# Logits turned one block later, and later loads spread over the run, in a float32 mixture-of-experts and mixing kernel on one core

## The chip, the cores and the metric

The kernel runs on one core of a Trainium2 chip. The metric is the device time of one execution in microseconds; less is better. Inputs and outputs are float32.

## The reference

x has 8 sequences of 512 tokens with 128 features. Three steps follow each other, each with a layer norm and a residual; the first and the third have the same weights.

```python
x = x + 0.5 * ffn(layernorm(x), centroids, expert_biases, Ws_up, Ws_down, W_up, W_down)
x = x + attn(layernorm(x), WB, WBf, w1, w2, b)
x = x + 0.5 * ffn(layernorm(x), ...)

def ffn(x, ...):                       # 64 experts, hidden width 64, 8 chosen
    shared = silu(x @ Ws_up) @ Ws_down
    aff = x @ centroids.T              # the logits
    idx = top_k(aff + expert_biases, 8)
    w = sigmoid(aff[idx]); w = w / (sum(w) + 1e-8)
    cw = zeros(T, E); cw[t, idx] += w  # weight of each expert for each token
    h = silu(einsum('td,edf->etf', x, W_up))
    y = einsum('etf,efd->etd', h, W_down)
    return shared + einsum('etd,te->td', y, cw)

def attn(u, WB, WBf, w1, w2, b):
    xf = u @ WB.T, but u itself at the first token
    xb = u @ WBf.T, but u itself at the last token
    gamma = sigmoid(xf @ w1.T + xb @ w2.T + b)
    return gamma * (xf + xb) + (1 - gamma) * u
```

## The kernel before

All experts are computed for all tokens. The work is a list of 16 items: layer 0 for sequences 0 to 7, then layer 1 (the mix of the reference's second step, and its third) for sequences 0 to 7. Each item has 32 pairs of experts, so there are 512 steps n, each called a block here, plus 25 in which only the down products are left. In a block the loop at L549 writes:

- the up product of pair n (`up`, L495): 128x128 weights of two experts with the 512 tokens, into one of four ph buffers in PSUM; ScalarE makes h of it by silu (L497). The products of blocks 5 and 7 go into the second PSUM pool, which y uses later (`SPARE`).
- a scaling (`scale`, L503) by VectorE of the h of 22, later 20, blocks ago with the cw of its two experts. cw comes from DRAM: for every group of four pairs two loads of 512 KB (L338), which repeat each expert's row over 64 partitions. Four groups have room (`CW_BUFS`); when a group's last pair is scaled, the load of the group four later is written.
- the down product of 25 blocks ago (`down`, L513), which sums into y. At two blocks of every second item the shared expert's products are added (L528).
- one step of `finish` (L453), by which VectorE turns the finished y by 32x32 blocks into yt (four rows of four transposes, L233) and adds it to x (L465).
- one step of `coming`, the preparation of the next item.

A preparation (`prep`, L343) is a generator; each `yield` ends what is written in one block. For layer 1 it begins with `mix` (L249): statistics and norm, four rows of transposes into mixt, `BEHIND` = 3 blocks of distance, two blocks with the mix products pfb (L277, L284), each followed by an addition on VectorE (L293) and a tanh, then the new x. For both layers follow the norm (POOL makes rstd, L202 and L203), four rows of transposes into ut, three blocks of distance, and the product sl (L369) of logits and shared hidden layer. VectorE copies the logits to lg (L378), ScalarE makes hsh by silu (L379). Two yields later TensorE turns lg into pa (L387), a block later VectorE writes biased and the largest eight (L394, L402), and in the next blocks the weights (L405 to L417), cw_sb in two rows of transposes and its store to DRAM as cw_t (L444). ScalarE's sigmoid of the logits (L398) needs another table than silu, so a table load stands ahead of it and one behind. Item 0 has no such rows: TensorE turns its weights (pc, L425), and ScalarE copies them.

`FIRST_PREP` says at which block of an item the preparation of the next one begins: 18 for an item of layer 0, 5 for one of layer 1. Whatever is left of it is written at block `LAST_PREP` = 5 of its own item (`run(coming)`), ahead of that block's up product.

All loads and stores go through SP's queue in the order in which they are written. Each engine works through its own instructions in the order written; semaphores hold it where operands are not there. The order across engines is the program's, as nothing reorders it. `load_rest` (L148) is written at block 14, behind the first four cw groups: the second half of the down weights, x of sequences 2 to 7, and the mix's matrices (wb, wbf, w12, w12c, b). `make_mix` (L178) turns those from the first block of item 2 on.

Of the kernel before, what the change touches and what calls it, by code (L numbers as in the profile page):

```python
# [23 lines left out]
SHRINK = 32  # L24
# [1 line left out]
CW_BUFS = 4  # L26
FIRST = 14
BEHIND = 3
FIRST_PREP = (18, 5)
LAST_PREP = 5  # L30
SPARE = (5, 7)
SHARED = (8, 16)

# [2 lines left out]
def macaron_kernel(  # L36
# [35 lines left out]
    B, T, D = x.shape  # L72
    E, _, F = w_up.shape
# [32 lines left out]
    def load_x(s, a=0, e=NT):  # L106
        src = x[s].rearrange("(n p) d -> p n d", p=P)
        nc.sync.dma_start(out=xs[s][:, a:e, :], in_=src[:, a:e, :])  # L108
# [19 lines left out]
    def load_down(e0, e1):  # L128
        nc.sync.dma_start(
            out=wdn[:, e0 // 2 : e1 // 2, :],  # L130
            in_=w_down[e0:e1].rearrange("(q two) f d -> (two f) q d", two=2),
        )
# [15 lines left out]
    def load_rest():  # L148

        for k in range(2):  # L150
            nc.sync.dma_start(out=wsdn[k * F : (k + 1) * F, :], in_=ws_down)
        load_down(E // 2, E)
        for s in range(2, B):
            load_x(s)
        nc.sync.dma_start(out=wb_sb, in_=wb)
        nc.sync.dma_start(out=wbf_sb, in_=wbf)
        nc.sync.dma_start(out=w12[:, 0, :], in_=w1[0].partition_broadcast(P))
        nc.sync.dma_start(out=w12[:, 1, :], in_=w2[0].partition_broadcast(P))
        with nc.allow_non_contiguous_dma(reason="two columns, once"):
            nc.sync.dma_start(out=w12c[:, 0:1], in_=w1.rearrange("o d -> d o"))  # L160
            nc.sync.dma_start(out=w12c[:, 1:2], in_=w2.rearrange("o d -> d o"))
        nc.sync.dma_start(out=b_bc, in_=b.partition_broadcast(P))

    def transposed(dst, src, rows):
        ps = ps_m.tile([P, 512], F32, tag="m", name="turn_ps")
        nc.tensor.transpose(ps[:, :rows], src, ident[:rows, :rows])
        nc.scalar.copy(dst, ps[:, :rows])
# [71 lines left out]
    def turned_by_blocks(dst, src):  # L239

        dst = dst.rearrange("f (n p) -> f n p", p=P)
        yield from blocks(
            lambda i, q: dst[quad(i), :, quad(q)],
            lambda i, q: src[quad(q), :, quad(i)],
            D // B32,
            P // B32,
        )
# [95 lines left out]
    def prep(i):  # L343

        layer, s = items[i]
        if layer == 1:
            yield from mix(s)

        parts = 2 if i == 0 else 1
        mv, rstd = stats(xs[s], f"f{i}", parts)  # L350
        yield
        u = normed(xs[s], mv, rstd, D, f"f{i}")
        ut = norm.tile([P, T], F32, tag="ut", name=f"ut{i}")
        if i == 0:
            turned(lambda a, e, ps: nc.scalar.copy(ut[:, a:e], ps), u, f"ft{i}", parts)
            yield
        else:
            yield
            yield from turned_by_blocks(ut, u)
            for _ in range(BEHIND):  # L360
                yield
        uts[i] = ut


        sl = ps_m.tile([P, 2, H], F32, tag="m", name=f"sl{i}")
        hsh = small.tile([P, H], F32, tag="hsh", name=f"hsh{i}")
        lg = route.tile([P, H], F32, tag="lg", name=f"lg{i}")
        for k in range(2):
            nc.tensor.matmul(  # L369
                sl[:, k, :],  # L370
                lhsT=wsl[:, k, :, :].rearrange("d a f -> d (a f)"),
                rhs=ut[:, k * H : (k + 1) * H],
                start=True,
                stop=True,
            )
        for k in range(2):
            at, other = slice(k * F, (k + 1) * F), slice((1 - k) * F, (2 - k) * F)
            nc.vector.tensor_copy(lg[at, :], sl[at, k, :])  # L378
            nc.scalar.activation(hsh[other, :], sl[other, k, :], AF.Silu)  # L379
        shared[i] = hsh  # L380
        yield
        yield


        aff = ps_m.tile([P, NT, E], F32, tag="m", name=f"pa{i}")
        for j in range(NH):
            nc.tensor.transpose(  # L387
                aff[:, 2 * j : 2 * j + 2, :].rearrange("p c e -> p (c e)"),
                lg[:, j * P : (j + 1) * P],
                ident,  # L390
            )
        yield
        biased = route.tile([P, NT, E], F32, tag="biased", name=f"biased{i}")
        nc.vector.tensor_tensor(  # L394
            biased, aff, bias_bc.unsqueeze(1).to_broadcast([P, NT, E]), ALU.add
        )
        sig = route.tile([P, NT, E], F32, tag="rsig", name=f"rsig{i}")
        nc.scalar.activation(sig, aff, AF.Sigmoid)  # L398
        top = route.tile([P, NT, 8], F32, tag="top", name=f"top{i}")
        left = route.tile([P, NT, E], F32, tag="left", name=f"left{i}")  # L400
        for j in range(NT):
            nc.vector.max(top[:, j, :], biased[:, j, :])  # L402
        yield
        for j in range(NT):
            nc.vector.match_replace(left[:, j, :], top[:, j, :], biased[:, j, :], LOWEST)  # L405
        yield

        cw = route.tile([P, NT, E], F32, tag="cw", name=f"cwtok{i}")
        nc.vector.tensor_tensor(left, left, biased, ALU.not_equal)
        nc.vector.tensor_tensor(cw, sig, left, ALU.mult)  # L410
        yield
        tot = small.tile([P, NT], F32, tag="tot", name=f"tot{i}")
        nc.vector.tensor_reduce(tot, cw, AX.X, ALU.add)
        nc.vector.tensor_scalar(tot, tot, EPS_W, None, ALU.add)
        inv = small.tile([P, NT], F32, tag="inv", name=f"inv{i}")
        nc.vector.reciprocal(inv, tot)
        nc.vector.tensor_tensor(  # L417
            cw, cw, inv.unsqueeze(2).to_broadcast([P, NT, E]), ALU.mult
        )
        yield  # L420
        cw_t = dram.tile([E, T], F32, tag="cw_t", name=f"cw_t{i}")
        if i == 0:
            pc = ps_m.tile([P, H], F32, tag="m", name=f"pc{i}")
            for j in range(NH):
                nc.tensor.transpose(  # L425
                    pc[:, j * P : (j + 1) * P],
                    cw[:, 2 * j : 2 * j + 2, :].rearrange("p c e -> p (c e)"),
                    ident,
                )
            cw_sb = route.tile([P, H], F32, tag="lg", name=f"cw_sb{i}")  # L430
            nc.scalar.copy(cw_sb, pc)
            nc.sync.dma_start(out=cw_t[:, :H], in_=cw_sb[:E, :])
            nc.sync.dma_start(out=cw_t[:, H:], in_=cw_sb[E:, :])
        else:
            cw_sb = route.tile([E, T], F32, tag="cw_sb", name=f"cw_sb{i}")
            to = cw_sb.rearrange("e (c j p) -> e j c p", j=NH, p=P)
            turn = cw.rearrange("p (j c) e -> p j c e", j=NH)
            yield from blocks(
                lambda e, q: to[quad(e), :, :, quad(q)],
                lambda e, q: turn[quad(q), :, :, quad(e)],  # L440
                E // B32,
                P // B32,
            )
            nc.sync.dma_start(out=cw_t, in_=cw_sb)  # L444
        cw_ts[i] = cw_t
# [93 lines left out]
    def run(work):  # L539
        for _ in work:  # L540
            pass

    total = len(items) * NP
    coming = prep(0)
# [4 lines left out]
    for n in range(total + DOWN_LAG):  # L549
        i, pair = divmod(n, NP)  # L550
        if n < total:
            if i == 0 and pair == FIRST:
                run(coming)
                for g in range(CW_BUFS):
                    load_cw(g)
                load_rest()
            if i > 0 and pair == 0:
                while i not in shared:
                    next(coming)
            if i > 0 and pair == LAST_PREP:  # L560
                run(coming)
            if i + 1 < len(items) and pair == FIRST_PREP[items[i + 1][0]]:
                run(coming)
                coming = prep(i + 1)
            up(n)

        nearer = min(max(0, n - SHRINK) // 2, SCALE_LAG - SCALE_END)
        while scaled < total and scaled <= n - SCALE_LAG + nearer:
            scale(scaled)
            scaled += 1  # L570
        if n >= DOWN_LAG:
            down(n - DOWN_LAG)
            if finishing and next(finishing[0], finishing) is finishing:
                finishing.pop(0)
        if n < total:
            next(coming, None)
        if i == 2 and n < total:
            next(mixing, None)
    for rest in finishing:
# [42 lines left out]
```

## Time and profile before

| | |
|---|---|
| Time, median of 3 runs | 951.88 us (951.79 to 952.08) |
| The profiled execution: time, span | 952.56 us, 950.8 us |
| TensorE, products | 931.5 us busy, 98% of the span |
| VectorE | 710.5 us, 75% |
| ScalarE | 367.0 us, 39% |
| DMA queue of the loads and stores | 71.0% of 16 engines' span |
| Up products, down products | 521.7 us, 518.9 us |
| Granted TensorE clock, mean | 0.999 |

The page counts a float32 product of 512 columns as two matmuls. Products overlap each other in the records, so the two groups' times add up to more than the span. The idle column of a row is what the engine stood still just before that row, with what released it. SPq is SP's queue of DMA issues; the length of such a row is the time that the issue took, not the transfer.

### The profile page before, as it was taken

The numbers are of one execution on the slowest core, as the hardware profiler recorded it, in microseconds if no ns is written. First come the engines' busy times: TensorE is split into PE (matmuls) and PEld (weight loads), VectorE is DVE, ScalarE is ACT, GpSimd is POOL, SyncE is SP. The second block draws the span as 40 slices with busy tenths as digits, with TensorE's granted clock in tenths as the row PEclk, the third lists the DMA queues.
The fourth block names the chain that finished last, engine by engine and source line by source line (L and its number), as shares of the span: only waits on it lengthen the run. The fifth ranks groups of instructions, "written<-read, shape, count | busy, mean of one in ns | idle before, by whom it ended". The sixth has DMA issues, their size and how long they took to land.

```text
span 950.8 us, 8411 instructions
## 1 busy us (share of the span) xinstructions
PE 931.5 (98%) x2353; PEld 423.6 (45%) x2353; DVE 710.5 (75%) x2018; ACT 367.0 (39%) x621; POOL 39.6 (4%) x65
## 2 busy tenths in 40 slices
PE   7999999999999999999999999999999999999998
PEld 3434444444444444444444444444444444444443
DVE  4646975849578394869979799797997979979463
ACT  6633434334343343433434334343343433434330
POOL 1000000000000000000000000000000000000000
PEclk9999999999999999999999999999999999999999
DMA  7999994866949568565676656776566765667953
GB/s 178 217 203 190 204 190 106 178 123 139 213 96 193 122 146 170 133 139 133 138 156 154 139 132 150 153 162 145 133 150 152 165 143 133 149 149 167 193 128 66
DMA packets 88991, 145.72 MB, mean 153 GB/s; under 512 B 9840, under 2 KB 21936, under 8 KB 88944
## 3 DMA queue, kind: packets, MB, share of 16 engines
q1 hardware_dynamic: 88944, 145.18, 71.0%
q8 instruction: 18, 0.29, 0.1%
q14 instruction: 29, 0.24, 0.1%
HBM read 140.97 MB, written 4.19 MB: 153 GB/s over the span
## 4 chain that ended last, share of the span: by engine, by line
PE 67%; DVE 20%; DMA 5%; issue 2%; SPq 2%; ACT 2%; POOL 1%; POOLq 0%; DVEq 0%; ACTq 0%
PE y L513 33%; PE ph L495 31%; DVE h L503 6%; DVE yt L233 5%; DVE ut L233 5%; DMA cw<-cw_t 4%; SPq L108 2%; DVE u_f L209 1%; PE y L528 1%; DVE x L309 1%; POOL rstd_f L203 1%; DVE x L319 1%; DVE lg L378 1%; DMA x<-in_L_attn_u_dram 1%; PE pfb L284 1%
## 5 line engine op out<-in xcount | busy, mean ns | idle before, releaser
L495 PE MATMUL ph<-ut,wup 128*128 128x512 f32 x1024 | 521.7, 595 | 0.0
L513 PE MATMUL y<-h,wdn 128*128 128x512 f32 x1024 | 518.9, 592 | 1.5 <-DVE h L503 1.5
L497 ACT ACTIVATE h<-ph 128x512 f32<-128x512 f32 x512 | 301.6, 596 | 455.5 <-PE ph L495 452.4
L503 DVE TENSOR_TENSOR h<-h,cw 128x512 f32<-128x512 f32 x512 | 337.1, 686 | 44.6 <-DMA cw<-cw_t 39.1
L513 PEld LDWEIGHTS y<-h,wdn 128*128 128x128 f32 x1024 | 194.5, 190 | 246.7 <-issue 211.6
L495 PEld LDWEIGHTS ph<-ut,wup 128*128 128x128 f32 x1024 | 191.0, 190 | 219.5 <-issue 214.7
L233 DVE STREAM_TRANSPOSE yt<-y 32x128 f32<-32x128 f32 x240 | 74.9, 312 | 82.1 <-PE y L513 78.6
L233 DVE STREAM_TRANSPOSE ut<-u_f 32x128 f32<-32x128 f32 x240 | 72.5, 302 | 3.7
L233 DVE STREAM_TRANSPOSE mixt<-u_mix 32x128 f32<-32x128 f32 x128 | 38.7, 302 | 2.2
L233 DVE STREAM_TRANSPOSE cw_sb<-cwtok 32x128 f32<-32x128 f32 x120 | 36.0, 300 | 1.7
L379 ACT ACTIVATE hsh<-sl 64x256 f32<-64x256 f32 x32 | 12.1, 379 | 57.6 <-DVE lg L378 57.6
L293 DVE SCALAR_TENSOR_TENSOR pfb<-u_mix,ident,pfb 128x129 f32<-128x129 f32 x16 | 5.7, 357 | 37.4 <-PE pfb L284 37.4
L209 DVE TENSOR_SCALAR u_f<-x,mv_f,rstd_f 128x128 f32<-128x128 f32 x64 | 17.9, 343 | 19.7 <-POOL rstd_f L203 19.7
L202 POOL TENSOR_SCALAR rstd_f<-mv_f 128x4 f32<-128x4 f32 (+1 forms) x17 | 8.7, 511 | 533.9 <-DVE mv_f L200 533.9
L398 ACT ACT_TABLE_LOAD x16 | 20.5, 1283 | 14.2 <-DVE biased L394 14.2
L378 DVE COPY lg<-sl 64x256 f32<-64x256 f32 x32 | 13.5, 422 | 15.8 <-PE sl L369 8.3
L497 ACT ACT_TABLE_LOAD x16 | 20.5, 1283 | 0.3
L369 PE MATMUL sl<-ut,wsl 128*128 128x256 f32 x64 | 17.3, 395 | 0.0
L203 POOL TENSOR_TENSOR rstd_f<-rstd_f,minus_half 128x4 f32<-128x4 f32 (+1 forms) x17 | 16.9, 993 | 1.4
L198 DVE BATCH_NORM_STATS2 st_f<-x 128x6 f32<-128x128 f32 x64 | 13.9, 278 | 4.0 <-DMA x<-in_L_attn_u_dram 4.0
L209 DVE TENSOR_SCALAR u_mix<-x,mv_mix,rstd_mix 128x128 f32<-128x128 f32 x32 | 8.9, 344 | 10.0 <-POOL rstd_mix L203 10.0
L369 PEld LDWEIGHTS sl<-ut,wsl 128*128 128x128 f32 x64 | 12.5, 198 | 8.3 <-issue 3.8
(70 smaller groups left out, 232.2 us busy)
## 6 DMA issues: line engine op xcount, KB each, us to landing
cw<-cw_t SPq DMA_DIRECT2D x256, 512.0 KB, 6.8
cw_t<-cw_sb SPq DMA_DIRECT2D x15, 128.0 KB, 5.3
x<-in_L_attn_u_dram SPq DMA_DIRECT2D x7, 256.0 KB, 6.8
out_dram<-x SPq DMA_DIRECT2D x7, 256.0 KB, 2.3
wdn<-in_L_ffn_W_down_dram SPq DMA_DIRECT2D x2, 512.0 KB, 5.9
wup<-in_L_ffn_W_up_dram SPq DMA_DIRECT2D x2, 256.0 KB, 3.9
wup<-in_L_ffn_W_up_dram SPq DMA_DIRECT2D x1, 512.0 KB, 6.5
x<-in_L_attn_u_dram SPq DMA_DIRECT2D x2, 128.0 KB, 2.1
```

Source lines behind the costliest of these rows:

```text
L108: nc.sync.dma_start(out=xs[s][:, a:e, :], in_=src[:, a:e, :])
L198: nc.vector.bn_stats(st[:, j, :], src[:, j, :])
L203: nc.gpsimd.tensor_tensor(rstd[:, at], rstd[:, at], minus_half[:, at], ALU.pow)
L209: nc.vector.tensor_scalar(u[:, j, :D], src[:, j, :], mv[:, j, 0:1], rstd[:, j : j + 1], ALU.subtract, ALU.mult,)
L233: nc.vector.transpose(dst(i, q), src(i, q))
L369: nc.tensor.matmul(sl[:, k, :], lhsT=wsl[:, k, :, :].rearrange("d a f -> d (a f)"), rhs=ut[:, k * H : (k + 1) * H], start=True, stop=True,)
L378: nc.vector.tensor_copy(lg[at, :], sl[at, k, :])
L398: nc.scalar.activation(sig, aff, AF.Sigmoid)
L495: nc.tensor.matmul(ph, lhsT=w, rhs=uts[i], start=True, stop=True)
L497: nc.scalar.activation(h, ph, AF.Silu)
L503: nc.vector.tensor_tensor(h, h, cw_tiles[group][:, g, :], ALU.mult)
L513: nc.tensor.matmul(ys[i], lhsT=wdn[:, pair, :], rhs=hs.pop(n), start=pair == 0 and i % 2 == 0, stop=pair == NP - 1,)
```

## The change

The logits are turned three blocks behind their product (`BEHIND`) instead of two, for all items but the first. Preparations in items of layer 1 begin at block 6 instead of 5, and what is left of a preparation is written at block 6. Item 0 has one more yield ahead of the turn of its weights. `load_rest` becomes a generator: at block 14 it writes the down weights and x of sequence 2 alone; from block 32 on it goes one step further at every fourth block: first wb and wbf, then w12, then w12c and b, then x of sequences 3 to 7, one each.

```diff
-FIRST_PREP = (18, 5)
-LAST_PREP = 5
+FIRST_PREP = (18, 6)
+LAST_PREP = 6
...
         load_down(E // 2, E)
-        for s in range(2, B):
-            load_x(s)
+        load_x(2)
+        yield
         nc.sync.dma_start(out=wb_sb, in_=wb)
         nc.sync.dma_start(out=wbf_sb, in_=wbf)
+        yield
         nc.sync.dma_start(out=w12[:, 0, :], in_=w1[0].partition_broadcast(P))
         nc.sync.dma_start(out=w12[:, 1, :], in_=w2[0].partition_broadcast(P))
+        yield
...
         nc.sync.dma_start(out=b_bc, in_=b.partition_broadcast(P))
+        for s in range(3, B):
+            yield
+            load_x(s)
...
         shared[i] = hsh
-        yield
-        yield
+        for _ in range(2 if i == 0 else BEHIND):
+            yield
...
         if i == 0:
+            yield
             pc = ps_m.tile([P, H], F32, tag="m", name=f"pc{i}")
...
-                load_rest()
+                loading = load_rest()
+                next(loading)
...
             if i > 0 and pair == LAST_PREP:
                 run(coming)
+                coming = iter(())
             if i + 1 < len(items) and pair == FIRST_PREP[items[i + 1][0]]:
-                run(coming)
                 coming = prep(i + 1)
...
             next(coming, None)
+        if n >= SHRINK and pair % 4 == 0:
+            next(loading, None)
```

## The prediction

> **What bounds the kernel now.** I read the page's busy shares first, then TensorE's waits, then the timelines around those waits.
>
> ```profile
> span 950.8 us, 8411 instructions
> PE 931.5 (98%) x2353; PEld 423.6 (45%) x2353; DVE 710.5 (75%) x2018; ACT 367.0 (39%) x621; POOL 39.6 (4%) x65
> ```
>
> TensorE sets the end, and what can be won is only its own pauses: at most 950.8 - 931.5 = 19.3 us by this row, part of them at the start and the end. Who causes them, in the list of TensorE's waits (total us, times, longest):
>
> ```profile
> PE pa L387 <- DVE lg L378: 6.7, 9, 1.0
> ...
> PE y L513 <- DVE h L503: 1.5, 1, 1.5
> ...
> PE pc L425 <- DVE cwtok L417: 0.8, 1, 0.8
> ```
>
> The first row is the turn of the logits, waiting for VectorE's copy of their product. One of those places, in the timelines of TensorE and VectorE:
>
> ```profile
> 505.53 1.02 PE L495 MATMUL ph<-ut,wup 128*128 128x512 f32 x2
> 506.39 1.02 PE L513 MATMUL y<-h,wdn 128*128 128x512 f32 x2
> 508.12 0.41 PE L387 MATMUL pa<-ident,lg 128*128 128x128 f32 x2 [0.70 <-DVE lg L378]
> ...
> 504.62 0.69 DVE L503 TENSOR_TENSOR h<-h,cw 128x512 f32<-128x512 f32 x1
> 505.33 1.32 DVE L233 STREAM_TRANSPOSE yt<-y 32x128 f32<-32x128 f32 x4
> 506.68 0.42 DVE L378 COPY lg<-sl 64x256 f32<-64x256 f32 x1
> 507.54 0.43 DVE L378 COPY lg<-sl 64x256 f32<-64x256 f32 x1 [0.45 <-ACT hsh L379]
> ```
>
> See three things. An up or a down product starts 0.86 us after the one before, so a block (one of each) is 1.72 us. After the down product of 506.39 the turn would start at 507.25; it starts at 508.12, so 0.87 us is lost, not the 0.70 of the idle column. And VectorE reaches the copies late, behind four rows of yt. Two other places, and the transfers behind the first of them:
>
> ```profile
> 61.32 1.02 PE L495 MATMUL ph<-ut,wup 128*128 128x512 f32 x2
> 63.80 1.13 PE L513 MATMUL y<-h,wdn 128*128 128x512 f32 x2 [1.46 <-DVE h L503]
> ...
> 63.05 2.50 DVE L503 TENSOR_TENSOR h<-h,cw 128x512 f32<-128x512 f32 x4 [10.49 <-DMA cw<-cw_t]
> ...
> 34.12 15.84 SPq L108 DMA_DIRECT2D x<-in_L_attn_u_dram  x6
> ...
> 54.43 5.40 SPq L338 DMA_DIRECT2D cw<-cw_t  x8
> ...
> 16.24 0.41 PE L425 MATMUL pc<-ident,cwtok 128*128 128x128 f32 x2 [0.83 <-DVE cwtok L417]
> ```
>
> Six x loads hold SP's queue from 34.12 to 49.96; with seven small loads behind them the fifth group of cw is issued only at 54.43 although its buffer has been free since about 35. VectorE waits 10.49 us for it, TensorE 1.46 us.
>
> **How the sums are made.** The idle column says 0.70 where starts say 0.87. The Trainium skill (Perfetto Trace Analysis, Identifying the Most-Contended Engine) says that busy time of matmuls is a poor measure of headroom, because they are pipelined. This trace shows it: a pair is booked at 1.02 us and starts every 0.86. By the idle column (6.7 + 1.5 + 0.8, and 0.8 of two small waits named below) the ceiling of this change is 9.8 us; by starts it is 11.8. I count by starts.
>
> **Part 1, the turn one block later (two, with its product, in layer 1).** In the changed program's order the layer-1 preparation starts at block 6 of a sequence instead of 5. The mix products, the statistics, the logits' product and VectorE's copies each come one block later, and the turn two: block 32 instead of 30. What waits go: eight layer-1 turns lose between 0.86 and 0.88 each, 6.97 us; the one of sequence 2 in layer 0 loses 101.97 - 100.79 = 1.18.
> Is the new time enough? VectorE is last held to TensorE at the second mix product: its row at 482.55 follows a wait of 1.66 us for pfb, and from there it works almost without pause to the end of the copies at 507.97. After the change this stretch starts one block, 1.72 us, later and holds the same twelve scalings. A ut row changes place with a yt row, which costs nothing in sum. The addition x<-yt (0.60 us to its successor) now stands ahead of the copies. So the copies end 1.72 + 0.60 = 2.32 us later, and the turn's natural place moves by two blocks, 3.44. Of the wait of 0.87 the difference of 1.12 takes all, and 0.25 us is spare. That is thin: each 0.1 us by which the chain is longer than I sum beyond this costs 8 x 0.1 us.
> What follows the turn also moves. The group after it (biased, max, weights, the two rows of cw_sb) starts behind four scalings, 2.2 us later than before, and the flush at block 6 then puts both cw_sb rows together. I find the mix statistics 1.6 us later where TensorE's own frame is 0.87 us later, so VectorE is 0.7 us more behind. It waits 2.01 us for the first mix product now, so 1.3 us stays and it is in step again. TensorE's own need there is mixt, finished at 476.13 for a product at 478.85: 2.7 us spare becomes 2.0. The scaled h is 6.3 us or more ahead of its down product through layer 1, so a lag of 0.7 us does not show. ScalarE's sigmoid with its two table loads (1.28 + 0.38 + 1.28 us) moves by two blocks too; it waits for biased about 1 us now and about 0.5 after, and the four ph buffers cover that now. The shared product in the next sequence's second block needs hsh: 4.6 us spare now, about 1.9 after. The cw_t store goes to SP about 2.2 us later, and the loads of the next sequence behind it too; the first is used at 548.33, having been issued at 526.38, so some 14 us cover it. In layer 0 VectorE waits for y, up to 16.5 us at a time, and no new wait arises.
>
> **Part 2, one more block before sequence 0's weights are turned (pc).** TensorE would be free at 15.25 and waits until 16.24. An up product, into the spare y buffer that is free, now fills 0.86 of that. ScalarE copies pc behind one more activation (0.5 us), so the first cw_t stores and the first cw loads come 0.3 to 0.5 us later. The first scaling has 2.99 us before its down product: less 0.86 and 0.5, still 1.6. Gain 0.86.
>
> **Part 3, the loads.** x3 to x7 and the seven small loads leave the place ahead of the fifth cw group. Five x loads landed 0.88 us apart (4.4 us), the small ones took 3.9 more, so the group lands about 55 instead of 63.03, while TensorE needs it at 61. The 1.62 us (63.80 - 62.18) go. The moved loads now lie between cw groups: per group 1.0 MB in about 5.0 us of transfer plus 0.9 for x, against 6.87 us that four blocks use, so the lead still grows. One second row of cw_sb now waits behind the scaling that needs this fifth group, so sequence 1's cw_t is stored near 57 us and lands behind the queue near 72 (before: 78.2); its first group lands near 80 and is needed near 90. w12c and b_bc (2.2 us) fall behind that group. Here a rule speaks against the change: the Trainium skill (DMA: Bandwidth & Descriptors, Rules for kernel authors) says to issue a DMA early and wait for it late. By the rule this part gains nothing and risks an exposed x load. By the trace early is what costs: x3, the first of the moved ones, landed at 50.9 and is first read at about 125; put behind the ninth cw group it lands near 87, still 37 us ahead. By the rule the total below is 1.62 smaller. I take the row.
>
> **Part 4, the mix's matrices.** At 107.36 and 110.13 TensorE loses 0.62 and 0.51 us, first to ScalarE's sigmoid, which came late because VectorE's biased was late (ScalarE waited 2.49 us). With VectorE on time the table work ends about when TensorE arrives. Bounds: nothing, or all 1.13; the late VectorE explains most of it, so I take 0.8.
>
> **Sum.** 6.97 + 1.18 + 0.86 + 1.62 + 0.8 = 11.4 us. The profiled execution took 952.56, so 941.1; the median of the runs shown is 0.7 lower, so 940.5.
>
> **Rivals.**
> 1. The copies are still late. For it: only 0.25 us is spare, in a stretch of 26 us of VectorE work. Against: the wait is equal to 0.02 us in all eight layer-1 sequences, so the stretch is regular. With the chain 0.5 us longer than summed, 8 x 0.25 = 2 us come back, 942.5; with 1 us longer, 6, 946.5. Chance 0.20.
> 2. The wait only changes place, to the mix products, and the kernel is slower: VectorE, which carries 50 of every 59 us in layer 1, falls further behind with the later weights and mixt is late. It decides from 2.7 us of extra lag (I sum 0.7). Each us beyond that costs 8 us; at 4.1 us of lag it eats the whole gain, at 4.5 the time is 940.5 + 8 x 1.8 = 954.9. Against: 2.0 us of margin, and VectorE's own waits for pfb, which put it in step once per sequence. Chance 0.04.
> 3. The loads starve VectorE as long as before (sequence 1's cw_t lands late, or x and the small loads hold up a cw group by 5 us). Then the y wait (1.62), the turn of sequence 2 (1.18) and the mix waits (0.8) come back in another place: 944.1. For it: SP's queue is served in order and full from 34 to 78 us. Against: 5 to 10 us between each landing worked out and its need. Chance 0.05.
> 4. The change doesn't do what it says, the flush at block 6 pulling the turn ahead: then nothing moves by over 0.2% (1.9 us, about what a measurement of this kernel can tell from no change). The changed order has the turn behind three full blocks, so I give 0.03, which also stands for small gains and losses that cancel.
> The forecast itself has the remaining 0.68.
>
> **Range.** Lowest: all of part 4 and a little from the regular pitch, 939.6. The top takes in most of rival 1: 945.0. Faster by over 0.2%: 0.93; within: 0.03; slower: 0.04.
>
> **What would show it.** Right: no row "pa <- lg" among TensorE's waits, pfb still waited for by VectorE, the y wait at 61 us gone and VectorE's longest cw wait under 6 us, the pc row without a wait near 16. Wrong: pa rows of 0.2 to 0.7 us in layer 1 (rival 1), rows of pfb waiting for mixt (rival 2), or a new y wait between 60 and 110 us (rival 3).

## The result, and the profile after

The changed kernel takes 940.24 us (median of 4 runs, 940.08 to 940.82) against 951.98 us; the ratio is 0.9878 (95% interval 0.9861 to 0.9895). A later measurement gave 940.71 us and 0.9879 (0.9863 to 0.9896). The prediction was 940.5.

Lines of the change moved the numbers: L495 is now L501, L513 is L519, L503 is L509, L387 is L392, L378 is L383, L233 is L238, L425 is L431, L338 is L343; in the kernels of the experiments they differ again by a few lines, and the names of the tiles tell the place. The page of the changed kernel begins so:

```profile
span 939.0 us, 8397 instructions
PE 929.4 (99%) x2353; PEld 424.5 (45%) x2353; DVE 709.0 (76%) x2018; ACT 365.8 (39%) x621; POOL 39.6 (4%) x65
```

TensorE's busy time fell by 2.1 us only, the time of the profiled execution by 11.7 (952.56 to 940.82): what went is standing still. In the list of TensorE's waits (total us, times, longest) the rows of pa, y, pc and two small ones of the mix are gone. Now it is, complete:

```profile
PE cent_ps L175 <- POOL rstd_f L207: 4.2, 1, 4.2
PE ps_ft L230 <- DVE u_f L214: 1.2, 2, 0.9
PE po L484 <- ACT yt L478: 0.5, 1, 0.5
```

Only the first 6 us and the tail are left. The place shown before, a layer-1 turn, in TensorE's and VectorE's timelines:

```profile
504.48 1.02 PE L519 MATMUL y<-h,wdn 128*128 128x512 f32 x2
505.33 0.38 PE L392 MATMUL pa<-ident,lg 128*128 128x128 f32 x2
505.55 1.02 PE L501 MATMUL ph<-ut,wup 128*128 128x512 f32 x2
...
502.25 0.69 DVE L509 TENSOR_TENSOR h<-h,cw 128x512 f32<-128x512 f32 x1
502.86 0.68 DVE L471 SCALAR_TENSOR_TENSOR x<-yt,x 128x512 f32<-128x512 f32 x1
503.58 0.42 DVE L383 COPY lg<-sl 64x256 f32<-64x256 f32 x1
504.44 0.43 DVE L383 COPY lg<-sl 64x256 f32<-64x256 f32 x1 [0.45 <-ACT hsh L384]
```

The turn starts 0.85 us after the down product, at the regular step. The copies end at 504.87, 0.46 us ahead of it. Where the turn had to wait it started 0.15 us after the copies' end (507.97 and 508.12 before), so 0.31 us is spare (0.46 - 0.15). And the loads, in the timelines of VectorE and of SP's queue:

```profile
57.08 0.69 DVE L509 TENSOR_TENSOR h<-h,cw 128x512 f32<-128x512 f32 x1 [5.07 <-DMA cw<-cw_t]
...
34.41 10.01 SPq L108 DMA_DIRECT2D x<-in_L_attn_u_dram  x1
44.52 3.84 SPq L343 DMA_DIRECT2D cw<-cw_t  x4
```

One x load instead of six stands ahead of the fifth group of cw. VectorE waits 5.07 us there instead of 10.49, and its h comes 4.1 us ahead of TensorE's need.

### The profile page after: what moved, and what is told of

It reads as the page before. It is cut to its first block, busy times and chain, and to the rows that moved or that the text cites. A ratio compares the mean times of both kernels' runs of the same rounds, so it can differ in the third digit from the quotient of the medians.

```text
span 939.0 us, 8397 instructions
## 1 busy us (share of the span) xinstructions
PE 929.4 (99%) x2353; PEld 424.5 (45%) x2353; DVE 709.0 (76%) x2018; ACT 365.8 (39%) x621; POOL 39.6 (4%) x65
## 4 chain that ended last, share of the span: by engine, by line
PE 99%; DMA 0%; POOL 0%; DVE 0%; issue 0%; ACT 0%
PE ph L501 47%; PE y L519 47%; PE sl L374 2%; PE y L534 1%; PE pfb L289 1%; PE pfb L282 1%; PE pa L392 0%; DMA x<-in_L_attn_u_dram 0%; POOL rstd_f L208 0%; PE po L484 0%; PE ps_ft L230 0%; DVE st_f L203 0%; POOL rstd_f L207 0%; DVE x L486 0%; ACT yt L478 0%
## 5 line engine op out<-in xcount | busy, mean ns | idle before, releaser
L501 PE MATMUL ph<-ut,wup 128*128 128x512 f32 x1024 | 522.0, 595 | 0.0
L519 PE MATMUL y<-h,wdn 128*128 128x512 f32 x1024 | 518.8, 592 | 0.0
L503 ACT ACTIVATE h<-ph 128x512 f32<-128x512 f32 x512 | 300.2, 597 | 451.9 <-PE ph L501 445.0
L509 DVE TENSOR_TENSOR h<-h,cw 128x512 f32<-128x512 f32 x512 | 335.9, 686 | 43.1 <-DMA cw<-cw_t 35.4
L519 PEld LDWEIGHTS y<-h,wdn 128*128 128x128 f32 x1024 | 194.6, 190 | 244.9 <-issue 201.9
L501 PEld LDWEIGHTS ph<-ut,wup 128*128 128x128 f32 x1024 | 191.1, 191 | 219.7 <-issue 213.8
L238 DVE STREAM_TRANSPOSE yt<-y 32x128 f32<-32x128 f32 x240 | 74.9, 312 | 76.2 <-PE y L519 72.6
L238 DVE STREAM_TRANSPOSE ut<-u_f 32x128 f32<-32x128 f32 x240 | 72.2, 301 | 3.6
L238 DVE STREAM_TRANSPOSE mixt<-u_mix 32x128 f32<-32x128 f32 x128 | 38.7, 302 | 2.0
L238 DVE STREAM_TRANSPOSE cw_sb<-cwtok 32x128 f32<-32x128 f32 x120 | 36.0, 300 | 1.5
L383 DVE COPY lg<-sl 64x256 f32<-64x256 f32 x32 | 13.5, 422 | 15.5 <-PE sl L374 8.1
```

Of the source, the lines that this page charges most:

```text
L238: nc.vector.transpose(dst(i, q), src(i, q))
L501: nc.tensor.matmul(ph, lhsT=w, rhs=uts[i], start=True, stop=True)
L503: nc.scalar.activation(h, ph, AF.Silu)
L509: nc.vector.tensor_tensor(h, h, cw_tiles[group][:, g, :], ALU.mult)
L519: nc.tensor.matmul(ys[i], lhsT=wdn[:, pair, :], rhs=hs.pop(n), start=pair == 0 and i % 2 == 0, stop=pair == NP - 1,)
```

## The experiments

Each kernel was timed beside the kernel before on the same chip (whose medians were 951.99 to 952.26 us).

**The turn alone.** The distance of three blocks and the preparations from block 6; `load_rest` and pc as before.

```diff
-FIRST_PREP = (18, 5)
-LAST_PREP = 5
+FIRST_PREP = (18, 6)
+LAST_PREP = 6
...
-        yield
-        yield
+        for _ in range(2 if i == 0 else BEHIND):
+            yield
```

> The turn's distance and the later start of the preparations alone; loads and pc as before. My theory: the eight layer-1 waits of 0.87 us go, with the 0.03 us that each turn after a wait is longer (7.2 us). Sequence 2's wait of 1.18 goes too, but the loads still starve VectorE, so the sigmoid ends near 108.6 us as before or later while TensorE comes 1.2 us earlier, and the mix waits grow by what was won: net about 0. So 944.5 to 945.5. Rival, that all nine turns and the mix waits hang on the distance alone: 951.98 - 8.4 - 1.2 = 942.4.

Measured: 945.75 us, ratio 0.9936 (0.9924 to 0.9949), a little above what I expected and far from the rival. No pa row is left. But the mix waits grew, and something I had not expected followed. The first line is the mix wait in the kernel before; then TensorE's timeline in this run, and below it stretches of two us, whose column after POOL is the granted clock:

```profile
108.09 0.38 PE L182 MATMUL gate_ps<-w12c,wb_sb 128*128 128x1 f32 x2 [0.45 <-ACT rsig L398]
...
105.18 0.27 PE L166 MATMUL turn_ps<-ident,wb_sb 128*128 128x128 f32 x1
107.44 0.38 PE L182 MATMUL gate_ps<-w12c,wb_sb 128*128 128x1 f32 x2 [1.98 <-ACT rsig L398]
107.68 1.10 PE L495 MATMUL ph<-ut,wup 128*128 128x512 f32 x2
108.62 1.46 PE L513 MATMUL y<-h,wdn 128*128 128x512 f32 x2
...
110.38 2.05 PE L495 MATMUL ph<-ut,wup 128*128 128x512 f32 x2
...
108.00:110.00 2.00, 2.00 (x5) 0.69 (x4) 1.90 (x5) 1.99 (x5) 0.00 (x0) 0.77 1.08 215
110.00:112.00 2.00, 2.00 (x6) 1.19 (x5) 1.88 (x7) 0.39 (x3) 0.00 (x0) 0.50 1.07 213
112.00:114.00 2.00, 2.00 (x5) 0.89 (x4) 1.90 (x6) 0.69 (x2) 0.00 (x0) 0.88 1.05 205
```

With the loads in their old place VectorE is still late here, so the sigmoid is too, and TensorE, which no longer waits for the turn, waits for the sigmoid instead: 1.98 us in place of 0.45. After that pause the clock fell to half for about 3.4 us: the product pair of 110.38 is booked at 2.05 us, its like in the kernel before (110.96) at 1.10, and from its start to the next up product it takes 2.84 us instead of 1.80. So in sequence 2 the distance alone wins nothing: the turn's 1.21 us are lost again at the mix, and more. The median is near my sum partly because another thing helped, in the profiled execution at least: the fifth cw group landed at 62.05 us instead of 63.03, and TensorE waited for y only 0.25 us instead of 1.46. The issues are the same in both kernels up to there, so I take that for a matter of the execution.

**The loads alone.** The generator of `load_rest` in the kernel before.

```diff
-        for s in range(2, B):
-            load_x(s)
+        load_x(2)
+        yield
...
+        for s in range(3, B):
+            yield
+            load_x(s)
```

> The spread loads alone. My theory: the y wait of 1.62 us goes, and because VectorE is no longer starved also sequence 2's turn wait (1.18) and both mix waits (1.2): 951.98 - 4.0 = 948.0. Rival, the sum of the prediction, in which sequence 2's turn hangs on the distance: only 1.62 and at most part of the mix waits, 949.5 to 950.4. Rival by the rule that early loads cost nothing: 952.0.

Measured: 948.13 us, ratio 0.9959 (0.9946 to 0.9973), my theory to 0.2 us. The row of pa has eight places in place of nine, each of the layer-1 size, and the rows of y and of the mix are gone:

```profile
PE pa L392 <- DVE lg L383: 5.5, 8, 0.7
```

By starts the wait for y gave 1.73 us, sequence 2's turn 1.21 and the mix 1.29. So sequence 2's turn and both mix waits hung on the cw loads. The prediction had put the first on the turn's distance.

**The yield ahead of pc alone.**

```diff
         if i == 0:
+            yield
             pc = ps_m.tile([P, H], F32, tag="m", name=f"pc{i}")
```

> The extra yield ahead of pc alone: 0.86 us, so 951.1. If the later cw_t store counted, the first scaling would lie on the path and it would be 951.98 or more.

Measured: 952.75 us, ratio 1.0010 (1.0002 to 1.0018): not faster, and rather slower. The wait for pc is gone as intended (first row; the row had an idle column of 0.83). The gain is lost at the next place that waits for a transfer:

```profile
17.32 0.41 PE L426 MATMUL pc<-ident,cwtok 128*128 128x128 f32 x2
...
61.54 1.02 PE L496 MATMUL ph<-ut,wup 128*128 128x512 f32 x2
64.31 1.13 PE L514 MATMUL y<-h,wdn 128*128 128x512 f32 x2 [1.74 <-DVE h L504]
```

There the fifth cw group sets the time, 63.80 before and 64.31 here. It landed at 63.54 instead of 63.03: the first stores of cw_t went out 1.57 us later (19.55 against 17.98), and the cw loads behind them landed 0.4 to 1.1 us later. Of the 1.57 us some 1.1 belong to this execution, whose third up product already started at 12.04 instead of 10.95; the rest, about 0.5, is what the yield itself moves. Why the median lies 0.7 us above that of the kernel before is not shown beyond this.

**The changed kernel without that yield.**

```diff
         if i == 0:
-            yield
             pc = ps_m.tile([P, H], F32, tag="m", name=f"pc{i}")
```

> The changed kernel without the extra yield ahead of pc. With that yield alone the gain was lost again at the y wait near 64 us, where the fifth cw group comes when it comes. My theory: with the loads spread that wait is gone, so here the yield counts: without it TensorE waits 0.83 us before pc and nothing gives it back: 0.86 us more, 941.1. Rival, that the yield is worth nothing in either surrounding: 940.2.

Measured: 941.57 us, ratio 0.9889 (0.9874 to 0.9904), 0.9 to 1.3 us above the changed kernel's two medians. TensorE's timeline has the old wait again, and no wait behind it:

```profile
16.67 0.41 PE L430 MATMUL pc<-ident,cwtok 128*128 128x128 f32 x2 [0.83 <-DVE cwtok L422]
```

The same yield is worth nothing while a transfer sets the time at 64 us, and about 0.9 us once it doesn't. The intervals of the two ratios overlap, so the medians alone do not show it. The traces do: between the third and the ninth up product the changed kernel gains 0.86 us on this one and keeps it to the end.

**The distance taken back.** The changed kernel with two yields before the turn.

```diff
-        for _ in range(2 if i == 0 else BEHIND):
+        for _ in range(2):
```

> The changed kernel with the turn again two yields behind its product; the later start of the preparations, loads and pc stay. My theory: the product, the copies and the turn come one block later, but x<-yt (0.60) now stands ahead of the copies, so each layer-1 turn waits 0.87 + 0.60 = 1.47 us, 11.8 us in all: 952.0, with eight rows pa <- lg. Rival, that the later start makes the gain and the distance none: 940.2 to 941.

Measured: 951.55 us, ratio 0.9993 (0.9985 to 1.0001). Everything else of the change together then wins nothing, though the loads alone won 4 us:

```profile
504.53 1.02 PE L519 MATMUL y<-h,wdn 128*128 128x512 f32 x2
506.77 0.41 PE L392 MATMUL pa<-ident,lg 128*128 128x128 f32 x2 [1.23 <-DVE lg L383]
```

The turn was due at 505.39 (504.53 + 0.86) and starts at 506.77: 1.38 us instead of the 0.87 before, eight times 11.0. The later start of the preparations is thus a loss by itself, since it puts x<-yt ahead of the copies, and it eats what the loads and pc win.

**The start at block 5, the distance kept.**

```diff
-FIRST_PREP = (18, 6)
-LAST_PREP = 6
+FIRST_PREP = (18, 5)
+LAST_PREP = 5
```

> The changed kernel with layer-1 preparations begun, and finished, at block 5 again; the turn stays three blocks behind. My theory: copies where they were, turn one block later than before: 1.72 - 0.87 = 0.85 us spare, more than the changed kernel's 0.3, and no wait in either: 940.2, within 0.4. Rival, that the later start is needed (the weights' rows or cw_t come too late otherwise): waits in layer 1, over 941.

Measured: 940.34 us, ratio 0.9874 (0.9859 to 0.9889), as the changed kernel. The copies and the turn:

```profile
501.19 0.43 DVE L383 COPY lg<-sl 64x256 f32<-64x256 f32 x1 [0.44 <-ACT hsh L384]
...
502.59 0.38 PE L392 MATMUL pa<-ident,lg 128*128 128x128 f32 x2
```

The copies end at 501.61 and the turn starts at 502.59: 0.98 us apart in place of 0.46, so 0.83 us is spare. The later start was not needed for the gain.

**One and two additions ahead of the copies.** VectorE is loaded in the changed kernel to see how much room there is.

```diff
+        for _ in range(1 if layer == 1 else 0):
+            nc.vector.scalar_tensor_tensor(spare, u, 0.5, xs[s], ALU.mult, ALU.add)
         for k in range(2):
             at, other = slice(k * F, (k + 1) * F), slice((1 - k) * F, (2 - k) * F)
             nc.vector.tensor_copy(lg[at, :], sl[at, k, :])
```

> The changed kernel with one addition of VectorE (128x512, 0.60 us to its successor, result unused) ahead of the logits' copies in layer 1. The copies end 0.32 us before they would hold the turn. My theory: 0.60 - 0.32 = 0.28 us of wait at each of eight turns, 2.2 us: 942.5. Rival, VectorE has room there: 940.2.

> As with one addition, but two. My theory: 1.20 - 0.32 = 0.88 us at each of eight turns: 7.0 us, 947.3. Rival: 940.2 to 941.

Measured: 942.81 us, ratio 0.9899 (0.9884 to 0.9914), and 948.89 us, ratio 0.9963 (0.9949 to 0.9977). TensorE's timeline with one addition, then with two:

```profile
503.70 1.02 PE L522 MATMUL y<-h,wdn 128*128 128x512 f32 x2
504.83 0.41 PE L395 MATMUL pa<-ident,lg 128*128 128x128 f32 x2
...
504.67 1.02 PE L522 MATMUL y<-h,wdn 128*128 128x512 f32 x2
506.54 0.41 PE L395 MATMUL pa<-ident,lg 128*128 128x128 f32 x2 [0.85 <-DVE lg L386]
```

With one the turn is 0.27 us late (504.83 against 504.56), as expected from 0.60 - 0.32. With two it is 1.01 us late where 0.88 was expected: from the first one's start to the copies it takes 1.45 us, not 1.20. Both write the same tile; whether that is why was not tried. Eight times 1.01 is 8.1 us; the median is 8.65 above that of the changed kernel, and the rest is within the spread of the runs (947.96 to 949.35). The spare time of the changed kernel is real, and as small as 0.3 us.

**Warm-up at the start.** The traces showed TensorE at half pace in the first us, with the step to full pace at another time in each execution. Unused turns of the identity were put ahead of its first work in the changed kernel, six at first:

```diff
+    warm_ps = ps_y.tile([P, 512], F32, tag="y", name="warm_ps")
+    for _ in range(6):
+        nc.tensor.transpose(warm_ps[:, :P], ident, ident)
```

> The changed kernel with six unused turns of the identity ahead of TensorE's first work, from about 1.5 us on. In the changed kernel's trace the first products run at half pace until 10.3 us (256 columns 0.43 us in place of 0.21, 512 columns 0.85 in place of 0.43). My theory: with TensorE busy since 1.5 us the full pace comes near 5 to 7 us, which wins up to 2.3 us; the first scaled h, which hangs on the transfers, gives 0.5 back: 938.4. If the pace did not hang on earlier work: 940.2.

Measured: 940.33 us, ratio 0.9874 (0.9859 to 0.9889): no gain. The six are booked at 1.54 us in all, TensorE stood still again for 0.93 us before the first real work, and the half pace lasted to 10.5 us. Then 14, and 7 more between the first turns:

```diff
+    keep_warm(14)
     turn_ps = ps_m.tile([P, 512], F32, tag="m", name="cent_ps")
...
+            keep_warm(5 if part == 0 else 2)
             ps = ps_m.tile([P, len(js) * P], F32, tag="m", name=f"ps_{name}_{part}")
```

> The changed kernel with 14 unused turns of the identity ahead of TensorE's first work, 5 more ahead of the first and 2 ahead of the second turn of sequence 0. Six turns took 1.3 us in all and the engine stood still again from 2.5 to 3.8, and the half pace lasted to 10.8 as without them. My theory: now TensorE works almost without pause from 1.3 us on, the full pace comes between 5 and 8 us, and 1.0 to 1.9 us are won: 938.3 to 939.3. Rival, that the start is bound by the loads and VectorE (the first down product has 1.9 us to spare at its least): what is won at the start is lost by 36 us, 940.2.

Measured: 939.16 us, ratio 0.9865 (0.9849 to 0.9882). To compare the two directly, both once more on one chip:

> The changed kernel once more, beside the one with the long warm-up, on one chip. Its full pace begins when the clock rises, which in ten traces so far was anywhere from 8.6 to 11.8 us without the warm-up: 940.0 to 941.0.

> The long warm-up once more. My theory: the clock rises 2 to 5 us earlier than without it and the time is 1.0 to 1.5 us under that of the changed kernel of this call. Rival, that the gain of 1.1 us was the luck of one call: equal within 0.4 us.

Measured: 940.71 us (940.42 to 940.98) and 939.20 us (939.00 to 940.08), 1.5 us apart. The first line is the product sl in the changed kernel, the others TensorE's timeline with the long warm-up:

```profile
6.90 1.91 PE L374 MATMUL sl<-ut,wsl 128*128 128x256 f32 x4
...
1.35 3.25 PE L178 MATMUL warm_ps<-ident 128*128 128x128 f32 x14 [1.35 <-POOL minus_half L102]
...
7.04 1.20 PE L382 MATMUL sl<-ut,wsl 128*128 128x256 f32 x4
8.07 1.45 PE L509 MATMUL ph<-ut,wup 128*128 128x512 f32 x3
```

The record of the clock begins, at full, at 6.6 us instead of 10.6; what the clock was ahead of that is told only by the pace of the products. The four records of sl take 1.20 us in place of 1.91. This version is faster than both kernels.

## Why the prediction was right, point by point

What each part won can be read from the starts of the same up products in the two profiled executions. That of the second block of the last item, for one, starts at 869.01 us before and at 857.36 after, 11.65 us earlier.

| Part | In the sum, us | By starts, us |
|---|---|---|
| Eight layer-1 turns | 6.97 | 7.21 |
| Sequence 2's turn | 1.18 | 1.21 |
| pc | 0.86 | 0.86 |
| The wait for y | 1.62 | 1.73 |
| The mix waits | 0.8 | 1.24 |
| A slower start | none | -0.58 |

The parts won 12.25 us, 0.8 more than the sum, over half of that at the mix; a slower start of this execution hid 0.6 of that. That the total came within 0.3 us is in part luck, and it says nothing on which edit won what. The runs above say that.

- **The layer-1 turns** (6.97 us). Right in cause and size. Taking the distance back brings the waits back (951.55). A turn after a wait is also about 0.03 us longer itself, which adds 0.2 us that I had not counted.
- **The spare time** (0.25 us). It is 0.31, and one addition of 0.60 us overdraws it by 0.27. The pace of the stretch was right too: from the second mix product's row to the end of the copies 25.95 us (478.92 to 504.87), worked out 26.0.
- **Cover behind the turn.** VectorE waits 1.35 us for the first mix product (1.3 worked out), mixt has 2.07 us to spare (2.0). The scaled h was not 6.3 us ahead at the least: I had read every fourth block, and the least in layer 1 was 5.0, now 4.25. It still hides the lag.
- **Sequence 2's turn** (1.18 us). The size was right, the step was not: I put it on the distance. The loads alone take the wait away, and the distance alone gives it back to the mix waits. That the sum came out all the same is luck of the bundle: the change has both edits.
- **pc** (0.86 us). Right in the changed kernel, but only there. Alone it gave nothing, because I priced it as if it stood by itself.
- **The loads** (1.62 us). Right for y. The group landed at 57.0 us, not 55; the need at 61 still had room. The first group of sequence 1 landed at 80.6 (worked out: near 80), x3 at 87.7 (near 87). Taken as it was, that an early issue costs nothing, the rule of the Trainium skill (DMA: Bandwidth & Descriptors, Rules for kernel authors) to issue a DMA early would have made 952.0 us of the loads alone; measured are 948.13. The early x loads cost the waits behind them, and no wait for the late ones shows.
- **The mix waits** (0.8 us). Too small: all of it went, 0.62 + 0.51 us and 0.1 in the short products between them. They were the loads' as well: together the loads are worth about 4 us (948.13), more than the 2.4 of y and mix in my sum.
- **Not in the sum:** the first up product started at 8.61 us instead of 8.35 and ran at half pace longer, which cost this profiled execution 0.6 us at the fifth up product (13.25 against 12.67). It is the same program up to there, so it is a matter of the execution.

The counting by starts was right. By the idle column the ceiling was 9.8 us; the time of the profiled execution fell by 11.7, and without its slower start it would have been about 12.3.

## What to carry to other kernels

Count a TensorE wait from start to start of its neighbours, not by its idle column, and price an edit behind the next wait in the program: a gain ahead of a transfer that sets the time is lost there until that wait is taken away too. Early loads in a queue served in order are not free when a transfer on the path is written behind them. When a step is given more distance, look at what else moves ahead of it: here one addition ate a third of a block, and the distance without the shift leaves more room for the same time.

## What the runs showed of the hardware that I had not expected

With the turn alone, a pause of 1.98 us was followed by half the TensorE clock (0.50 from 110 to 112 us, about 3.4 us long), while pauses of 1.46 and 1.74 us in the profiled executions of the kernel before and of pc's yield alone were not. The Trainium skill (TensorE: Matmul & The Clock Gate, Why this matters for your kernels) advises against idle gaps over about 3 us; in this trace 2 us was enough once. The yield alone may have met it too, in executions that were not profiled: seven of its 13 were granted 0.996 or 0.997 in the mean, and one of the 25 of the kernel before beside them. The clock also falls behind the last product, where nothing is lost; in the profiled executions that takes 0.0013 of the mean at most (2.5 us at half), so it is not the whole of it.

In the records of the clock the changes lie whole steps of 3.413 us apart: with the turn alone the clock is full for 98.99 us (29 steps), half for one step; in the kernel before it is full for 938.67 us (275), in the changed one for 928.43 (272). Of the pause of 1.98 us, 1.78 lie within one such step, more than half of it; of the other two it is 1.46 and 1.36. That fits a clock which goes by the idle share of one step, so that the same pause can cost or not by where it falls. Three pauses do not show a threshold.

At the start the half pace ended at 9.7 us in the kernel before, at 10.6 in the changed one, at 11.8 with pc's yield alone and at 8.6 with one addition, with the same work ahead of it. The same page (Part 1) says that the window is free-running, which fits: these times spread over 3.1 us, less than one step. The starts differ by about 1.6 us at the fifth up product (12.17 to 13.76) for reasons outside the program. Without a warm-up, a difference of that size between single profiles of this kernel can come from the start alone.
